# Two states of a scan summed on GpSimd, experts summed in one PSUM bank, and a routing result turned one step later

## The chip, the cores and the metric

The kernel runs on one core of a Trainium2 chip. Its time is device time in microseconds (us) of one execution; three runs of the kernel before gave 5223.3 to 5244.32 us with a median of 5229.83 us. The profile is one further execution. A core has TensorE (PE, matrix products, which write to the accumulator memory PSUM), VectorE (DVE), ScalarE (ACT), GpSimd (POOL) and SyncE (SP, which here issues the DMA transfers). They work side by side, each through its own list of instructions in order, and wait for one another on semaphores. SBUF is the working memory on the chip.

## What is computed

The input x has the shape (4, 128, 64, 64) in fp32: four images of 128 channels and 4096 pixels. Layer 0 normalises, convolves, and runs a selective scan over the pixels of each image. The scan has 16 states for each of its inner channels:

```python
dA = jnp.exp(delta[..., None] * A)
dBu = delta[..., None] * Bm[:, :, None, :] * xin[..., None]
def step(h, inp):
    dA_t, dBu_t, C_t = inp
    h = dA_t * h + dBu_t
    y = jnp.einsum('bdn,bn->bd', h, C_t)      # sum over the 16 states n
    return (h, y)
y = jnp.transpose(ys, (1, 0, 2)) + D_skip * xin
out = y * jax.nn.silu(z) @ out_proj_w.T
```

Layer 1 is attention over the 4096 pixels of an image with 4 heads, followed by a mixture of 8 experts of which the two most probable count:

```python
router_probs = jax.nn.softmax(x @ router_w + router_b, axis=-1)
top_p, top_i = jax.lax.top_k(router_probs, K)                     # K = 2
top_p = top_p / jnp.sum(top_p, axis=-1, keepdims=True)
expert_out = jnp.einsum('bnd,edc->bnec', x, expert_w) + expert_b
gathered = jnp.take_along_axis(expert_out, top_i[..., None], axis=2)
return jnp.einsum('bnk,bnkc->bnc', top_p, gathered)               # added to t
```

## The kernel before

**Tiling.** An image is cut into 8 blocks of 512 pixels (`BLK`, `NB`). Channels lie on the 128 partitions, pixels along the free dimension. For the scan a block has two halves `p` of its channels, and each half has 8 *units* of two states each (`n = 0, 2, ..., 14`): 4 x 8 x 2 x 8 = 512 units. All engine calls go through a helper that keeps the order in which they are written, so nearly every instruction carries line 467 in the profile; the tile names tell them apart.

**The main loop** (line 1322 on) goes in *steps*, called `slot` in the code; a unit takes two, so the scan takes 1024. In the even step of a unit VectorE makes `h<-rows,du` (`driven`, the input of both states, 128x1024) and then the scan `h<-da,state,h` (128x1025, both states in one instruction). In the odd step it makes `hc<-rows,h` (`read`): both states times their row of C. What is left is the sum over the states. It is taken in PSUM: `turned_on` (line 824) turns a term by four transposes of 128x128 on PE, and all terms of a half block are accumulated in the one bank `y`, states and units alike. The list `due` says when: the first term of a unit at the step after its product (`slot + 1`; for the first unit of a half two steps later), the second at `slot + 2`. After the last term ScalarE copies `y`, PE turns it back (`turned_back`), and `summed_up` gates it.

**Attention beside it.** In each step PE also makes the scores `sc<-qs,ks` of one group of keys (four matmuls) and the weighted sums `av<-pT,v` of the group before, and ScalarE makes two exponentials `pT<-sc` of 128x1024. Attention of an image starts as soon as its blocks are closed and outlasts the scan.

**Two lanes.** Everything else is written as generators which are advanced by two stages in each step: lane X runs `closed` (the end of layer 0 of a block) and `finished` (the end of layer 1 of a block, with the experts: an *output*), lane Y runs the norms, the convolution `conv` and `inputs` (the projections that feed the scan). A `yield` ends a stage. Each lane has one PSUM bank, `ps_X` and `ps_Y` (`work(lane)`); `inputs` uses both, and the set `held` says so. An output is started only in certain steps of a block.

**The output** (`finished`, line 1087). After routing on VectorE, whose result is `both` (the shares of the 8 experts, plain and scaled), PE turns `both`, ScalarE copies it to `prT`, and the scaled shares go to DRAM and come back broadcast over the partitions (`share`, two experts at a time, 512 KB). Before the change, `eb8` (the experts' biases times the shares) is made by a matmul in the bank, added with `xf` into `res` on VectorE, and then for every two experts PE makes two matmuls in the bank and VectorE adds the bank to `res`: five VectorE additions of 128x512 an output. There are 32 outputs.

**In steps that are short of work** a stage that must be done by now is forced by `until`, which advances both lanes outside the step order.

Of the kernel before, what the change touches and what calls it, by code (L numbers as in the profile page):

```python
# [24 lines left out]
NST = 16  # L25
DH = 32
NH = 4
NE = 8
# [8 lines left out]
def conv_mamba_attn_moe_kernel(ctx: ExitStack, tc: tile.TileContext, t: dict):  # L37
# [435 lines left out]
    def mm(out, lhsT, rhs, start=True, stop=True):  # L473
        tensor.matmul(out, lhsT=lhsT, rhs=rhs, start=start, stop=stop)
# [8 lines left out]
    def send(out, in_, slots=1):  # L483
        outgoing.append([slots, out, in_])
# [24 lines left out]
    def work(lane, shape=None):  # L509
        return ps_work.tile(shape or [P, BLK], F32, tag=f"work{lane}", name=f"ps_{lane}")  # L510

    def tmp(lane, name, shape=None):
        return side.tile(
            shape or [P, BLK], F32, tag=f"tmp{lane}", name=name, bufs=6 if lane == "X" else 4
        )
# [197 lines left out]
    def inputs(b, i, p):  # L713

        xn, pairs = xn_of[b, i], pairs_of[b, i]
        r = slice(DI * p, DI * p + DI)
        while held:
            yield
            yield
        held.add("in")  # L720
        ps = work("Y")
        summed(ps, [(inxc[:, j, :], pairs[:, p, 2 * j : 2 * j + BLK]) for j in range(2)])
        pz = work("X")
        mm(pz, inz[r, :], xn[r, 3 : 3 + BLK])
        yield
        xin = mix.tile([P, BLK], F32, name="xin", bufs=2)
        scalar.activation(xin, ps, AF.Silu, bias=cb)
        zs = mix.tile([P, BLK], F32, name="zs", bufs=4)
        scalar.activation(zs, pz, AF.Silu)
        yield  # L730

        pb = work("X")
        mm(pb[0:DI, :], wbc, xin)
        ps = work("Y")
        mm(ps, wdt, xin)
        yield
        held.clear()
        bc = tmp("Y", "bc")[0:DI, :]
        scalar.copy(bc, pb[0:DI, :])
        bcd = dram.tile([2, NST // 2, 2, 2 * BLK], F32, name="bcd", bufs=4)  # L740
        send(bcd.rearrange("c n k (m q) -> (c n k m) q", m=2), bc)

        e = tmp("Y", "e")
        scalar.activation(e, ps, AF.Abs, bias=dtb)
        scalar.activation(e, e, AF.Exp, scale=-1.0)
        ln = tmp("Y", "ln")
        scalar.activation(ln, e, AF.Ln, bias=1.0)
        delta = mix.tile([P, BLK], F32, name="delta", bufs=2)
        scalar.activation(delta, ps, AF.Relu, bias=dtb)
        yield  # L750
        yield

        du = mix.tile([P, BLK], F32, name="du", bufs=2)
        lost = du
        vector.tensor_scalar(lost, e, 1.0, -1.0, ALU.add, ALU.add)
        vector.tensor_sub(lost, e, lost)
        vector.tensor_add(ln, ln, lost)
        vector.tensor_add(delta, delta, ln)
        vector.tensor_mul(du, delta, xin)
        in_of[b, i, p] = xin, zs, delta, du, bcd  # L760
        done.add(("in", b, i, p))
        yield
# [324 lines left out]
    def finished(b, qb, lane):  # L1087

        q, u = divmod(qb, 2)
        td = kqv[b][3]  # L1090
        s = slice(qb * BLK, (qb + 1) * BLK)
        acc = side.tile([P, NT, C], F32, name="acc", bufs=2)
        aT, inv = tmp(lane, "aT"), tmp(lane, "inv")
        sync.dma_start(out=aT, in_=total[b, q][u, 0].rearrange("h d q -> (h d) q"))
        sync.dma_start(
            out=inv, in_=inverse[b, q][u][:, None, :].to_broadcast([NH, DH, BLK])
        )
        sync.dma_start(out=acc.rearrange("p j c -> p (j c)"), in_=td[:, s])
        yield
        yield  # L1100
        yield
        vector.tensor_mul(aT, aT, inv)
        yield
        ps = work(lane, [P, NT, C])
        for j in range(NT):
            mm(ps[:, j, :], aT[:, j * P : (j + 1) * P], wp)
        yield
        vector.tensor_add(acc, ps, acc)
        rs = spread(lane, acc)
        yield  # L1110
        ps = transposed(lane, acc)
        yield
        xf = tmp(lane, "xf")
        scalar.copy(xf, ps)
        yield
        ps = work(lane, [P, NT, NE])
        for j in range(NT):
            mm(ps[:, j, :], xf[:, j * P : (j + 1) * P], rw)
        wide = [P, NT, NE]

        def routed(name, n=NE):
            return small.tile([P, NT, n], F32, name=f"{name}{lane}", bufs=1)

        yield

        both = routed("both", 2 * NE)
        pr = routed("pr")
        vector.tensor_mul(pr, ps, rs[:, :, None].to_broadcast(wide))
        vector.tensor_add(pr, pr, rb[:, None, :].to_broadcast(wide))
        m = routed("m", 1)  # L1130
        vector.tensor_reduce(m, pr, AX.X, ALU.max)
        vector.tensor_sub(pr, pr, m.to_broadcast(wide))
        yield
        yield
        scalar.activation(pr, pr, AF.Exp)
        yield
        yield

        revb = rev[:, None, :].to_broadcast(wide)

        def largest(src, tag):
            top, f, pick = routed(f"top{tag}", 1), routed(f"f{tag}", 1), routed(f"pick{tag}")
            vector.tensor_reduce(top, src, AX.X, ALU.max)
            vector.tensor_tensor(pick, src, top.to_broadcast(wide), ALU.is_equal)
            vector.tensor_mul(pick, pick, revb)
            vector.tensor_reduce(f, pick, AX.X, ALU.max)
            vector.tensor_tensor(pick, pick, f.to_broadcast(wide), ALU.is_equal)
            return top, pick

        top1, pick1 = largest(pr, 1)  # L1150
        rest = routed("rest")
        vector.scalar_tensor_tensor(rest, pick1, -2.0, pr, ALU.mult, ALU.add)
        top2, pick2 = largest(rest, 2)
        vector.tensor_add(pick1, pick1, pick2)
        vector.tensor_mul(pr, pr, pick1)
        vector.tensor_add(top1, top1, top2)
        vector.reciprocal(top1, top1)
        vector.tensor_mul(both[:, :, 0:NE], pr, top1.to_broadcast(wide))
        vector.tensor_mul(both[:, :, NE:], both[:, :, 0:NE], rs[:, :, None].to_broadcast(wide))
        yield  # L1160

        ps = work(lane)
        for j in range(NT):
            tensor.transpose(ps[0 : 2 * NE, j * P : (j + 1) * P], both[:, j, :], ident)
        yield
        prT = tmp(lane, "prT")[0 : 2 * NE, :]
        scalar.copy(prT, ps[0 : 2 * NE, :])
        shares = dram.tile([NE, BLK], F32, name=f"shares{lane}")
        send(shares, prT[NE:, :])
        yield  # L1170

        def share(e):

            if lane == "X":
                w = side.tile([P, 2, BLK], F32, name="share", bufs=3)
            else:
                w = mix.tile([P, 2, BLK], F32, tag="rows", name="share", bufs=4)
            sync.dma_start(
                out=w.rearrange("p k q -> p (k q)"),
                in_=shares[e : e + 2].rearrange("e q -> (e q)")[None].to_broadcast([P, 2 * BLK]),  # L1180
            )
            return w


        ps = work(lane)
        mm(ps, eb8, prT[0:NE, :])
        yield
        res = tmp(lane, "res")
        vector.tensor_add(res, ps, xf)
        yield  # L1190
        ahead = deque(share(e) for e in (0, 2))
        yield
        yield
        for e in range(0, NE, 2):
            if e + 4 < NE:
                ahead.append(share(e + 4))
            yield
            w = ahead.popleft()
            if e:
                vector.tensor_add(res, res, ps)  # L1200
            vector.tensor_mul(w, w, xf[:, None, :].to_broadcast([P, 2, BLK]))
            yield
            ps = work(lane)
            for u in range(2):
                mm(ps, ew[:, e + u, :], w[:, u, :], u == 0, u == 1)
        yield
        vector.tensor_add(res, res, ps)
        send(out[b][:, s], res, 2)
        yield


# [86 lines left out]
    groups = attention_groups()  # L1298
    units = [(b, i, p, n) for b, i in blocks for p in range(2) for n in range(0, NST, 2)]
    END = 2 * len(units)  # L1300

    rows, due, closing, y_of = {}, deque(), deque(), {}
    h_of, slot = {}, 0
# [18 lines left out]
    while (  # L1322
# [23 lines left out]
        if unit and odd:  # L1346
            hc = read(h, rows.pop((at, 1)))
            late = 2 * (unit[3] == 0)
            due.append((slot + 1 + late, unit, 0, hc[:, 0, :], False))
            due.append((slot + 2, unit, 1, hc[:, 1, :], ends(unit)))  # L1350
        advance("Y", False)
        while closing and closing[0][0] <= slot:
            summing = turned_back(*closing.popleft()[1:])
# [133 lines left out]
```

## Time and profile before

| | us |
|---|---|
| median of three runs | 5229.83 |
| lowest, highest run | 5223.3, 5244.32 |
| profiled execution, its own time | 5221.24 |
| span of the profile | 5219.4 |

The page has a row for each kind of instruction: how many there were, then their busy time together and the mean duration of one, then the idle time of the engine just before them and what ended it. These rows matter here:

```profile
L467 PE MATMUL y<-ident,hc 128*128 128x128 f32 x4096 | 626.6, 284 | 64.9 <-DVE hc L467 64.9
L467 DVE TENSOR_TENSOR hc<-rows,h 128x1024 f32<-128x1024 f32 x512 | 624.2, 1219 | 16.1 <-PE y L467 5.9
L467 DVE TENSOR_TENSOR res<-res,ps_X 128x512 f32<-128x512 f32 x108 | 73.7, 682 | 51.9 <-PE ps_X L467 51.5
L467 PE MATMUL ps_X<-share,w_ew 128*128 128x512 f32 x432 | 215.5, 622 | 8.7 <-DVE share L467 8.5
```

A matmul's own duration (284 ns for a transpose) is longer than the spacing of two of them, because they are pipelined; 626.6 us for 4096 transposes make 153 ns each. The second part of the page cuts the span into 40 slices of 130 us and gives the busy share of each engine in tenths:

```profile
PE   4566898999999999899999999999999999999997
DVE  4888767777788877888788877888788877751332
ACT  3456787788777777688887787788777787756543
POOL 1111101100000000001000000000000001000000
```

The first slices are the scan of the first blocks, for which there is no attention yet; the scan ends at about 4620 us (the last `y<-ident,hc` starts at 4620.1), and after it attention runs alone, to 5152 us, with the last outputs behind it.

### The profile page before, as it was taken

What the parts mean: (1) busy time and instruction counts of PE and PEld (TensorE: products, weight loads), DVE (VectorE), ACT (ScalarE), POOL (GpSimd) and SP (SyncE); (2) the same over time, 40 slices, a digit from 0 to 9 for tenths busy, and PEclk for the clock granted to TensorE, in tenths of its full rate; (3) what the DMA queues carried; (4) which work ended last, traced back from release to release, by engine and by line L of the source; (5) the groups of instructions that cost most, each with busy time, mean ns of one, the idle gap of its engine ahead of it and who ended that gap; (6) DMA issues with size and microseconds to landing.
All of it is one profiled execution on the core that took longest, in us unless ns stands there. A gap on an engine that the chain in (4) does not pass through costs nothing.

```text
span 5219.4 us, 62693 instructions
## 1 busy us (share of the span) xinstructions
PE 4743.5 (91%) x20704; PEld 2300.7 (44%) x20704; DVE 3834.5 (73%) x5809; ACT 3749.8 (72%) x5701; POOL 423.5 (8%) x483
## 2 busy tenths in 40 slices
PE   4566898999999999899999999999999999999997
PEld 2333444444444444444444444444444444443443
DVE  4888767777788877888788877888788877751332
ACT  3456787788777777688887787788777787756543
POOL 1111101100000000001000000000000001000000
PEclk8677999999999999899999999999999999999998
DMA  3556667767776667767766667767766666754542
GB/s 96 188 186 202 206 215 247 232 231 238 244 231 218 227 227 243 238 232 246 260 230 231 224 223 230 262 227 259 259 236 227 215 230 226 263 181 153 184 134 72
DMA packets 451694, 1131.62 MB, mean 217 GB/s; under 512 B 51985, under 2 KB 135330, under 8 KB 451362
## 3 DMA queue, kind: packets, MB, share of 16 engines
q1 hardware_dynamic: 450194, 1126.74, 64.3%
q8 instruction: 166, 2.72, 0.2%
q14 instruction: 166, 1.36, 0.1%
q10 hardware_dynamic: 1168, 0.80, 0.1%
HBM read 967.12 MB, written 143.39 MB: 213 GB/s over the span
## 4 chain that ended last, share of the span: by engine, by line
PE 55%; DVE 18%; ACT 13%; DMA 6%; issue 5%; POOL 2%; SPq 1%; DVEq 0%; ACTq 0%; POOLq 0%
PE av L467 23%; PE sc L467 13%; PE ps_X L467 8%; DVE h L467 6%; PE ps_Y L467 5%; PE y L467 5%; ACT pT L467 4%; ACT L467 3%; DMA ks<-kd 2%; DVE hc L467 2%; ACT xt L467 1%; ACT e L467 1%; DMA rows<-bcd 1%; DVE stX L467 1%; POOL rsX L467 1%
## 5 line engine op out<-in xcount | busy, mean ns | idle before, releaser
L467 ACT ACTIVATE pT<-sc 128x1024 f32<-128x1024 f32 x2048 | 1984.8, 1023 | 940.1 <-PE sc L467 938.4
L467 PE MATMUL av<-pT,v 128*64 128x512 f32 x8192 | 1998.3, 609 | 12.4 <-DVE avs L467 12.4
L467 PE MATMUL sc<-qs,ks 128*128 128x512 f32 x4096 | 1296.1, 436 | 64.4 <-DMA ks<-kd 32.7
L467 DVE TENSOR_TENSOR_SCAN h<-da,state,h 128x1025 f32<-128x1025 f32 x512 | 1204.2, 2352 | 90.0 <-ACT h L467 56.2
L467 PEld LDWEIGHTS sc<-qs,ks 128*128 128x128 f32 x4096 | 701.3, 190 | 793.3 <-ACT pT L467 261.7
L467 PEld LDWEIGHTS av<-pT,v 128*64 128x64 f32 x8192 | 499.5, 137 | 844.4 <-issue 813.8
L467 ACT ACTIVATE da<-delta,amat 128x512 f32<-128x512 f32 x1024 | 743.0, 730 | 1.9
L467 PE MATMUL y<-ident,hc 128*128 128x128 f32 x4096 | 626.6, 284 | 64.9 <-DVE hc L467 64.9
L467 DVE TENSOR_TENSOR hc<-rows,h 128x1024 f32<-128x1024 f32 x512 | 624.2, 1219 | 16.1 <-PE y L467 5.9
L467 DVE TENSOR_TENSOR h<-rows,du 128x1024 f32<-128x1024 f32 x512 | 623.4, 1218 | 14.2 <-DMA rows<-bcd 13.7
L467 PEld LDWEIGHTS y<-ident,hc 128*128 128x128 f32 x4096 | 520.6, 147 | 235.7 <-issue 83.9
L467 ACT ACT_TABLE_LOAD x319 | 409.3, 1283 | 19.5 <-DVE zs L467 14.3
L467 POOL TENSOR_TENSOR rsX<-rsX,mhalf 128x4 f32<-128x4 f32 x92 | 203.8, 2216 | 2524.6 <-DVE rsX L467 2440.5
L467 POOL TENSOR_TENSOR rsY<-rsY,mhalf 128x4 f32<-128x4 f32 x100 | 130.4, 1304 | 2071.0 <-DVE shiftY L467 1560.3
L467 DVE TENSOR_TENSOR avs<-av,prev 128x512 f32<-128x512 f32 x96 | 66.1, 689 | 252.9 <-PE av L467 238.3
L467 PE MATMUL ps_X<-share,w_ew 128*128 128x512 f32 x432 | 215.5, 622 | 8.7 <-DVE share L467 8.5
L467 ACT ACTIVATE xt<-ps_Y,shiftY,rsY 128x128 f32<-128x128 f32 x380 | 143.8, 469 | 106.4 <-POOL shiftY L467 99.0
L467 DVE TENSOR_TENSOR share<-share,xf 128x1024 f32<-128x1024 f32 x128 | 155.9, 1218 | 15.6 <-DMA share<-sharesX 9.9
L467 ACT COPY state<-h 128x2 f32<-128x2 f32 x448 | 88.7, 198 | 93.5 <-DVE h L467 93.5
L467 DVE SCALAR_TENSOR_TENSOR cm<-y,w_fc1w,cm 128x512 f32<-128x512 f32 x192 | 142.8, 744 | 3.4
L467 PE MATMUL ps_Y<-pairs,inxc 128*128 128x512 f32 x256 | 129.2, 629 | 15.6 <-DMA pairs<-xn 10.3
L467 PEld LDWEIGHTS ps_X<-share,w_ew 128*128 128x128 f32 x432 | 73.6, 190 | 146.8 <-issue 98.5
(254 smaller groups left out, 3455.8 us busy)
## 6 DMA issues: line engine op xcount, KB each, us to landing
rows<-bcd SPq DMA_DIRECT2D x1024, 512.0 KB
ks<-kd SPq DMA_DIRECT2D x192, 512.0 KB
qs<-qd SPq DMA_DIRECT2D x161, 512.0 KB
share<-sharesX SPq DMA_DIRECT2D x108, 512.0 KB
v<-vd SPq DMA_DIRECT2D x192, 256.0 KB
ks<-kd SPq DMA_DIRECT2D x128, 256.0 KB
avd<-avs SPq DMA_DIRECT2D x96, 256.0 KB
prev<-avd SPq DMA_DIRECT2D x96, 256.0 KB
```

What stands on the lines that cost most here:

```text
L467: return lambda *args, **kw: queued(op(*args, **kw))
```

## The change

The edit has three parts.

1. *Two states.* From step 64 on (`ALONE = NB // 2 * NST`), GpSimd adds the two halves of the product `hc` in place, a 128x512 addition, and PE turns and accumulates one term for each unit instead of two. The term is due at `slot + 2` (for the first unit of a half at `slot + 3`). In the first 64 steps all is as before. So 480 of the 512 units have the addition.
2. *Experts in one bank.* The bias matmul `eb8` and the eight experts' matmuls are accumulated in one PSUM bank in one go; VectorE adds `xf` once at the end. Between the first and the last of them lane X keeps its bank: it puts `"mix"` into `held`, for which `inputs` waits, and before it does so it waits itself until `held` is empty.
3. *Shares later.* Two more stages, one step, lie between the routing on VectorE and the transposes of its result on PE.

```diff
@@ inputs @@
-        held.clear()
+        held.discard("in")
@@ finished @@
         vector.tensor_mul(both[:, :, NE:], both[:, :, 0:NE], rs[:, :, None].to_broadcast(wide))
         yield
-
+        yield
+        yield
         ps = work(lane)
...
-        ps = work(lane)
-        mm(ps, eb8, prT[0:NE, :])
-        yield
-        res = tmp(lane, "res")
-        vector.tensor_add(res, ps, xf)
+        yield
         yield
         ahead = deque(share(e) for e in (0, 2))
         yield
         yield
+        while lane == "X" and held:
+            yield
+            yield
+        if lane == "X":
+            held.add("mix")
+        ps = None
         for e in range(0, NE, 2):
             if e + 4 < NE:
                 ahead.append(share(e + 4))
             yield
             w = ahead.popleft()
-            if e:
-                vector.tensor_add(res, res, ps)
             vector.tensor_mul(w, w, xf[:, None, :].to_broadcast([P, 2, BLK]))
             yield
-            ps = work(lane)
+            if e == 0:
+                ps = work(lane)
+                mm(ps, eb8, prT[0:NE, :], True, False)
             for u in range(2):
-                mm(ps, ew[:, e + u, :], w[:, u, :], u == 0, u == 1)
-        yield
-        vector.tensor_add(res, res, ps)
+                mm(ps, ew[:, e + u, :], w[:, u, :], False, e + u == NE - 1)
+        yield
+        res = tmp(lane, "res")
+        vector.tensor_add(res, ps, xf)
         send(out[b][:, s], res, 2)
+        held.discard("mix")
         yield
@@ main loop @@
+    ALONE = NB // 2 * NST
...
             late = 2 * (unit[3] == 0)
-            due.append((slot + 1 + late, unit, 0, hc[:, 0, :], False))
-            due.append((slot + 2, unit, 1, hc[:, 1, :], ends(unit)))
+            if slot < ALONE:
+                due.append((slot + 1 + late, unit, 0, hc[:, 0, :], False))
+                due.append((slot + 2, unit, 1, hc[:, 1, :], ends(unit)))
+            else:
+                gpsimd.tensor_add(hc[:, 0, :], hc[:, 0, :], hc[:, 1, :])
+                due.append((slot + 2 + late // 2, unit, 0, hc[:, 0, :], ends(unit)))
```

## The prediction

> **What bounds the kernel now.** I read four views in this order: the page's first table, the busy table cut into stretches of one block, the waits inside those stretches, and the timeline of GpSimd against VectorE.
>
> ```profile
> PE 4743.5 (91%) x20704; PEld 2300.7 (44%) x20704; DVE 3834.5 (73%) x5809; ACT 3749.8 (72%) x5701; POOL 423.5 (8%) x483
> ```
>
> TensorE (PE) leads, but an average over the span cannot say what an edit is worth. A block of 512 pixels is 16 units of the scan (two halves of eight). I cut the block that begins at 2708.30 at the starts of its products hc: two units, seven units, seven units.
>
> ```profile
> 2708.30:2734.13 25.83, 25.83 (x116) 12.59 (x116) 13.21 (x19) 22.96 (x33) 0.00 (x0) 1.00 0.54 182
> 2734.13:2796.05 61.92, 59.78 (x273) 29.39 (x270) 58.99 (x93) 44.63 (x74) 5.07 (x8) 1.00 0.66 225
> 2796.05:2853.20 57.15, 55.73 (x257) 26.82 (x256) 45.42 (x67) 49.50 (x77) 6.54 (x6) 1.00 0.71 233
> ```
>
> Columns: stretch, length, then busy us of PE, weight loads, DVE (VectorE), ACT, POOL (GpSimd). In the first and third stretch PE is busy 100% and 97.5% of the time and VectorE 51% and 79%: PE sets the time. In the middle one both are full, VectorE at 95%, PE at 97%. The waits agree; the first two lines below are VectorE's from the first stretch, the next from the middle one (PE's), the last two from the third:
>
> ```profile
> DVE acc L467 <- PE ps_X L467: 8.5, 1, 8.5
> DVE xin L467 <- PE y L467: 2.7, 1, 2.7
> ...
> PE ps_X L467 <- DVE bothX L467: 2.1, 1, 2.1
> ...
> DVE hi L467 <- PE ps_X L467: 5.8, 2, 3.4
> DVE vst L467 <- PE ps_X L467: 3.3, 1, 3.3
> ```
>
> Outside the middle stretch VectorE runs ahead and waits for PE. Inside it VectorE's listed waits are only 1.3 us (0.7 for a res, 0.6 for a cm), and PE waits 2.1 us for the routing result bothX. The middle stretch is therefore VectorE's: what loads VectorE there lengthens it, and what relieves PE there gains nothing.
>
> **The one thing the trace must tell: GpSimd against VectorE.** The new add reads two SBUF operands on GpSimd. The kernel before has no such add, but it has small GpSimd operations beside large VectorE ones:
>
> ```profile
> 2605.96 0.24 POOL L467 COPY y<-y 128x64 f32<-128x64 f32 x1
> ...
> 1149.38 1.15 POOL L467 COPY y<-y 128x64 f32<-128x64 f32 x1
> ...
> 1149.22 1.22 DVE L467 TENSOR_TENSOR h<-rows,du 128x1024 f32<-128x1024 f32 x1
> ...
> 2807.55 1.99 POOL L467 TENSOR_TENSOR rsX<-rsX,mhalf 128x4 f32<-128x4 f32 x1 [1.96 <-DVE shiftX L467]
> ...
> 2807.45 1.22 DVE L467 TENSOR_TENSOR hc<-rows,h 128x1024 f32<-128x1024 f32 x1
> 2808.59 1.22 DVE L467 TENSOR_TENSOR h<-rows,du 128x1024 f32<-128x1024 f32 x1
> ```
>
> The same copy takes 0.24 us alone and 1.15 us when h<-rows,du is running: it ends 0.09 us after that product. The power 128x4 takes 1.01 us alone (at 4636.01) and 1.99 us when it meets hc. Since 0.87 us of it follow hc's end while the next product is already started, GpSimd gets in between two VectorE instructions that follow each other.
>
> [...] that VectorE waits for GpSimd no instruction of this trace shows[...]. [...] COPY 128x64 at 0.24 and COPY 128x3 at 0.18 us make 0.98 ns an element, twice that for two operands, so 1.0 us and 0.18 of start. I take a hold of 1.1 us, with ends 0 (VectorE is not held) and 1.9 us.
>
> **The change part by part.**
>
> The sum of two states. 480 of the 512 units (all but the first 64 steps, 32 units) lose four transposes. At 2741.07 four of them start and the next av starts at 2741.60, so 0.53 us of PE a unit (busy time says 626.6/4096 x 4 = 0.61, ends overlapping). In the first and third stretch, PE's own, that is 9 x 0.53 = 4.8 us a block. VectorE has room there: it is busy 13.2 + 45.4 of 83.0 us, and nine holds add at most 9.9. In the middle stretch the 3.7 us of PE are worth nothing.
>
> There the hold counts. I laid one add behind each of the seven hc of that stretch in the timeline[...]: behind du<-e 1.1; behind gn [...] 0.8; behind h, delaying the scan, 1.0; beside the first tap cm 0.65; then 1.05 three times, delaying a tap or an h. Sum 6.7 us on a VectorE without slack.
>
> The term is due at step +2 instead of +1 and +2. The add is done 1.2 to 2.3 us after hc, a step lasts 145/32 = 4.5 us, so PE's transposes do not wait; if that cover went, each late add would cost PE its lateness. Powers queued behind an add need statistics which VectorE makes after hc anyway (4 x 0.28 us and more): nothing, or up to 1.1 us each on ACT's xt where this fails. The product buffer hc is freed at the same step +2.
>
> Experts in one bank. For each of the 32 outputs VectorE loses five 128x512 adds and gains one. In the middle stretch: res<-ps_X,xf 0.69 and four res<-res,ps_X 2.7 go, one 0.69 comes, and the 0.7 wait before the first goes: 3.4 us off VectorE. PE's matmuls are the same; eb8 moves behind the first share. The bank is held by lane X during the mix and the `inputs` stage waits for it: in the instruction order of the two kernels the matmuls of `inputs` stand at the same step or one earlier, so nothing waits.
>
> Shares a step later. Two stages more between routing and transposes. It takes away PE's 2.1 us for bothX (45.9 us over the span), but in VectorE's stretch: 0, at most those 46 us. One extra step of lane X has room.
>
> **Sum for a block with an output:** middle 6.7 - 3.4 - 0.6 (the wait for PE at its end) = +2.7; others -4.8; together -2.1. For 23 such blocks -48. Five blocks (554 to 1244 us) have no output and so no adds to lose; there VectorE has 4.5 of 60.0 us idle to take up the holds (1127.90 to 1187.89): +4 - 4.8 = -0.8 each, -4. The two blocks between 310 and 554 us, where PE is busy 72% and VectorE 81%: 0 to +25, I take +11. The tail: both last outputs run eb8 (2.07 and 1.91 us at 5190.79 and 5192.66) before the shares arrive, now after: +3. Total -38 us: 5221.2 - 38 = 5183 against the profiled execution, which is 8.6 us under the median; so 5192 for the median.
>
> **Rivals.**
>
> A. VectorE is hardly held [...]. Then the middle stretch follows PE, which loses 3.7 and 2.1, and VectorE, which loses 3.4: -3.2; others -4.8; -8.0 in 23 blocks, about -6.8 in the five without an output, tail +3: -215, 5015. For it: no VectorE instruction in the trace is seen held. Against it: GpSimd is held fully in the other direction.
>
> B. Slower: the add holds VectorE longer than estimated, because it is slower itself or because each delayed VectorE instruction also delays its next partner. Place: the middle stretch; price: 6.7 x hold/1.1. The sum of a block changes sign at 6.7 x hold/1.1 = 4.8 + 4.0, a hold of 1.44 us. At 1.9 us it is +11.6 - 4.0 - 4.8 = +2.8 in 23 blocks (+64), +4.1 in the five others (+20), +20 at the start, +3 at the tail: 5337. For it: 95% busy VectorE with nothing to absorb. [...]
>
> C. The add comes late and PE waits for it, so that the unit is as long as before: half of the 4.8 us is gone in 28 blocks, 67 us: 5259. For it: PE waits for hc today, 64.9 us over the span. Against it: two steps of slack.
>
> **How the numbers follow.** Main case 0.50 (holds of 0.9 to 1.45 us give -3.3 to 0 a block, with the other terms -75 to +25 us: 5155 to 5255), A 0.17, B 0.24, C 0.09. A measurement of this kernel can tell about 0.5%, 26 us, from no change. Faster: 0.31 of the main case and all of A, 0.48; slower: B, 0.07 of C and 0.04 of the main case, 0.35; the rest, 0.17, within. Since both signs hold much, the main case's range stands above; the range for 8 in 10 reaches into A and B, 5050 to 5290.
>
> **What would show it.** Four transposes a unit fewer (about 2176 y<-ident,hc instead of 4096) and a new POOL row hc<-hc x480 at 1.1 us alone, 1.5 to 2.5 us with its wait. VectorE rows such as scan, h or the taps longer, or idle before them released by POOL, some 0.8 us a unit: if these are unchanged and the stretches of 62 us get shorter, A. PE's share in the middle stretch falls to about 88% and the stretch grows to 64 or 65 us; the rest of a block shrinks from 83.0 to 78 us. PE waits for bothX vanish. I am wrong if the middle stretch passes 67 us (B) or PE's waits for POOL before y exceed some 50 us (C).

## The result and the profile after

The change makes the kernel slower by 1.0%: 5286.18 us (5280.59 to 5287.42) against 5235.17 us for four runs of the kernel before (5223.3 to 5244.32; three of them are those of the section on the time before), ratio 1.0097 with a 95% interval of 1.0073 to 1.0121. The profiled execution has a span of 5283.8 us, 64 us more than before.

The first table of the page after the change:

```profile
PE 4630.3 (88%) x18784; PEld 2103.8 (40%) x18784; DVE 4039.5 (76%) x5681; ACT 3752.7 (71%) x5701; POOL 1350.8 (26%) x963
```

PE did lose its work: 1920 matmuls and 113 us. VectorE has 128 instructions fewer and yet 205 us more. The groups of instructions say where those come from (columns: count, then busy us in total and ns of one, then idle us before):

```profile
L467 POOL TENSOR_TENSOR hc<-hc 128x512 f32<-128x512 f32 x480 | 868.3, 1809 | 2294.1 <-DVE hc L467 2207.4
L467 DVE TENSOR_TENSOR_SCAN h<-da,state,h 128x1025 f32<-128x1025 f32 x512 | 1349.2, 2635 | 70.0 <-ACT h L467 36.6
L467 DVE TENSOR_TENSOR h<-rows,du 128x1024 f32<-128x1024 f32 x512 | 689.8, 1347 | 6.7 <-DMA rows<-bcd 6.7
L467 DVE SCALAR_TENSOR_TENSOR cm<-y,w_fc1w,cm 128x512 f32<-128x512 f32 x192 | 185.6, 967 | 3.4
L467 PE MATMUL y<-ident,hc 128*128 128x128 f32 x2176 | 355.9, 293 | 66.7 <-DVE hc L467 36.9
L467 PE MATMUL ps_X<-share,w_ew 128*128 128x512 f32 x432 | 235.2, 670 | 45.7 <-DVE share L467 45.6
```

Before, the scan took 2352 ns, h<-rows,du 1218 and the tap cm 744. Of VectorE's idle time only 15.9 us are put down to GpSimd, and 11.9 before: a VectorE instruction that is held shows as a longer one, not as a wait. One unit of the middle stretch shows it, first on VectorE's timeline (start, duration), then on GpSimd's:

```profile
3394.90 1.22 DVE L467 TENSOR_TENSOR h<-rows,du 128x1024 f32<-128x1024 f32 x1
3396.23 3.17 DVE L467 TENSOR_TENSOR_SCAN h<-da,state,h 128x1025 f32<-128x1025 f32 x1
3399.60 1.22 DVE L467 TENSOR_TENSOR hc<-rows,h 128x1024 f32<-128x1024 f32 x1 [0.20 <-POOL y L467]
3400.74 0.54 DVE L467 TENSOR_SCALAR cm<-y,w_fc1w,w_fc1b 128x512 f32<-128x512 f32 x1
3401.32 1.66 DVE L467 SCALAR_TENSOR_TENSOR cm<-y,w_fc1w,cm 128x512 f32<-128x512 f32 x1
```

```profile
3395.13 2.12 POOL L467 TENSOR_TENSOR hc<-hc 128x512 f32<-128x512 f32 x1 [3.50 <-DVE hc L467]
...
3400.91 1.52 POOL L467 TENSOR_TENSOR hc<-hc 128x512 f32<-128x512 f32 x1 [1.48 <-DVE hc L467]
```

The first addition starts while h<-rows,du runs and ends at 3397.25, 1.13 us after that product (3396.12); it takes 2.12 us, where the shortest of the 480 takes 1.26. The scan, started 0.11 us after the product, takes 3.17 us instead of 2.35. The second addition meets the tap cm, which takes 1.66 us instead of 0.74. The tap with one tile operand ahead of it keeps its 0.54 (all 24 of the span take 0.52 to 0.54).

Now the stretches of one block (columns as in the prediction, then PE's clock, DMA share, GB/s): first the kernel before, then the same block after.

```profile
3307.93:3329.53 21.60, 21.60 (x99) 10.56 (x99) 13.20 (x19) 20.88 (x29) 0.00 (x0) 1.00 0.75 210
3329.53:3391.47 61.94, 59.75 (x273) 29.40 (x270) 58.98 (x93) 43.97 (x67) 5.07 (x8) 1.00 0.64 217
3391.47:3448.18 56.71, 55.36 (x256) 26.66 (x254) 45.43 (x68) 48.61 (x70) 6.51 (x7) 1.00 0.69 233
```

```profile
3352.56:3372.87 20.31, 20.17 (x86) 9.34 (x88) 14.92 (x21) 19.04 (x27) 5.63 (x7) 1.00 0.59 191
3372.87:3437.81 64.94, 60.07 (x245) 27.32 (x242) 60.99 (x87) 44.84 (x68) 19.42 (x15) 0.95 0.62 219
3437.81:3498.71 60.90, 59.08 (x254) 26.48 (x254) 50.84 (x70) 52.85 (x76) 19.67 (x14) 1.00 0.69 225
```

The middle stretch is 3.0 us longer, as forecast. The third, which should have become shorter, is 4.2 us longer, and PE is busier in it by 3.7 us although it turns seven terms less: work has come into it from elsewhere. In the middle stretch PE has 28 instructions fewer, is busy no less, and its clock has sunk to 0.95.

This 0.95 comes from two short pieces at half the clock. Here is the first, on PE's timeline and then as a stretch of its own (columns as above):

```profile
3388.39 1.94 PE L467 MATMUL av<-pT,v 128*64 128x512 f32 x8
...
3393.23 0.66 PE L467 MATMUL ps_Y<-ident,xt 128*128 128x128 f32 x4 [1.77 <-ACT xt L467]
3393.81 3.39 PE L467 MATMUL av<-pT,v 128*64 128x512 f32 x8
```

```profile
3394.16:3397.56 3.40, 3.40 (x11) 0.77 (x8) 3.30 (x3) 3.10 (x6) 2.43 (x4) 0.50 0.36 117
```

PE waits 1.77 us for xt; ahead of the statistics for this xt VectorE had an h<-rows,du that took 2.30 us (at 3384.24) instead of 1.22. About 0.9 us after the wait PE's clock is at half for 3.41 us, and the eight matmuls of av take 3.39 us instead of 1.94. The second piece, from 3414.63 on, follows a wait of 2.17 us for an expert's share. In the 22 blocks of the table at the end, PE's time at half clock is 236 us after the change and 89 before.

PE's waits after the change:

```profile
PE sc L467 <- DMA ks<-kd: 56.7, 28, 6.0
PE sc L467 <- ACT pT L467: 54.3, 137, 2.6
PE ps_X L467 <- DVE share L467: 45.6, 17, 4.8
...
PE y L467 <- POOL hc L467: 28.3, 6, 8.4
```

The waits for bothX are down to 8.8 us from 45.9, and the one for the experts' shares has come (8.5 before). PE's wait for the added term is small, 28.3 us.

### The profile page after: what moved, and what is told of

The parts are those of the page before. It is cut to its first block, busy times and chain, and to the rows that moved or that the text cites. A ratio compares the mean times of both kernels' runs of the same rounds, so it can differ in the third digit from the quotient of the medians.

```text
span 5283.8 us, 59904 instructions
## 1 busy us (share of the span) xinstructions
PE 4630.3 (88%) x18784; PEld 2103.8 (40%) x18784; DVE 4039.5 (76%) x5681; ACT 3752.7 (71%) x5701; POOL 1350.8 (26%) x963
## 3 DMA queue, kind: packets, MB, share of 16 engines
q1 hardware_dynamic: 450194, 1126.74, 63.6%
## 4 chain that ended last, share of the span: by engine, by line
PE 47%; DVE 23%; ACT 12%; DMA 7%; issue 7%; POOL 2%; SPq 1%; DVEq 0%; POOLq 0%; ACTq 0%
PE av L467 20%; PE sc L467 11%; DVE h L467 10%; PE ps_X L467 8%; PE ps_Y L467 5%; ACT pT L467 4%; ACT L467 3%; DMA ks<-kd 3%; DVE hc L467 3%; PE y L467 3%; DVE cm L467 1%; ACT xt L467 1%; DVE du L467 1%; DVE stX L467 1%; SPq L467 1%
## 5 line engine op out<-in xcount | busy, mean ns | idle before, releaser
L467 PE MATMUL av<-pT,v 128*64 128x512 f32 x8192 | 2024.7, 616 | 40.5 <-DVE avs L467 40.2
L467 POOL TENSOR_TENSOR hc<-hc 128x512 f32<-128x512 f32 x480 | 868.3, 1809 | 2294.1 <-DVE hc L467 2207.4
L467 PE MATMUL sc<-qs,ks 128*128 128x512 f32 x4096 | 1320.0, 441 | 113.2 <-DMA ks<-kd 56.7
L467 DVE TENSOR_TENSOR_SCAN h<-da,state,h 128x1025 f32<-128x1025 f32 x512 | 1349.2, 2635 | 70.0 <-ACT h L467 36.6
L467 DVE TENSOR_TENSOR h<-rows,du 128x1024 f32<-128x1024 f32 x512 | 689.8, 1347 | 6.7 <-DMA rows<-bcd 6.7
L467 ACT ACT_TABLE_LOAD x319 | 409.3, 1283 | 21.1 <-DVE zs L467 15.9
L467 PE MATMUL y<-ident,hc 128*128 128x128 f32 x2176 | 355.9, 293 | 66.7 <-DVE hc L467 36.9
L467 POOL TENSOR_TENSOR rsY<-rsY,mhalf 128x4 f32<-128x4 f32 x100 | 148.6, 1486 | 1037.1 <-DVE shiftY L467 552.0
L467 PEld LDWEIGHTS y<-ident,hc 128*128 128x128 f32 x2176 | 292.2, 152 | 187.3 <-issue 62.0
L467 PE MATMUL ps_X<-share,w_ew 128*128 128x512 f32 x432 | 235.2, 670 | 45.7 <-DVE share L467 45.6
L467 DVE SCALAR_TENSOR_TENSOR cm<-y,w_fc1w,cm 128x512 f32<-128x512 f32 x192 | 185.6, 967 | 3.4
```

The lines of the kernel that those rows point to most:

```text
L467: return lambda *args, **kw: queued(op(*args, **kw))
```

## The experiments

Times are medians; those of the kernel before, measured beside the four sets, were 5237.7, 5236.7, 5238.5 and 5233.2. "Middle" is units 2 to 8 of a block, "outer" units 0, 1 and 9 to 15. The table at the end gives the mean lengths of both.

**First set: which part costs?**

*The additions alone*: the main loop of the change, with `finished` and `inputs` as before. Of the parts put back:

```diff
-        yield
-        yield
         ps = work(lane)
...
+        mm(ps, eb8, prT[0:NE, :])
...
+            if e:
+                vector.tensor_add(res, res, ps)
...
-                mm(ps, ew[:, e + u, :], w[:, u, :], False, e + u == NE - 1)
+                mm(ps, ew[:, e + u, :], w[:, u, :], u == 0, u == 1)
```

> GpSimd's sum of the two states alone, the experts and their shares as before the change. Theory H (each GpSimd add holds VectorE up[...]): VectorE gets the holds without the additions it loses in the changed kernel, so slower than the changed kernel, 5310 to 5360 us. Theory M (the mix in one bank and the shares a step later cost the time, TensorE waiting for the first share): the add shows its gain of about 4.8 us a block, 5080 to 5150 us. Theory L (TensorE gets its term too late from GpSimd, whatever VectorE does): about as the changed kernel, 5280 us, with TensorE waiting for GpSimd's hc.

5291.22 us, ratio 1.0097 (1.0075 to 1.0118). The additions by themselves give the whole loss, and theory M falls. The number is nearest to theory L's, but PE waits only 16.8 us for GpSimd's hc; H had the direction and too much of it.

*The experts' edits alone*: the main loop of before with the two other parts.

```diff
-            if slot < ALONE:
-                due.append((slot + 1 + late, unit, 0, hc[:, 0, :], False))
-                due.append((slot + 2, unit, 1, hc[:, 1, :], ends(unit)))
-            else:
-                gpsimd.tensor_add(hc[:, 0, :], hc[:, 0, :], hc[:, 1, :])
-                due.append((slot + 2 + late // 2, unit, 0, hc[:, 0, :], ends(unit)))
+            due.append((slot + 1 + late, unit, 0, hc[:, 0, :], False))
+            due.append((slot + 2, unit, 1, hc[:, 1, :], ends(unit)))
```

> Experts in one bank and shares a step later alone, two terms for a unit as before the change. H: VectorE loses about 2.7 us a block and nothing holds it, TensorE's wait for bothX is gone: faster than before by 20 to 90 us, 5145 to 5215. M: slower than before by 50 us or more, 5285 and up. L: as H.

5246.3 us, ratio 1.0017 (1.001 to 1.0023). No theory had that: 80 us less of VectorE (3754.2) bring no time. The same block shows where they go:

```profile
3319.07:3340.24 21.17, 21.04 (x94) 10.20 (x96) 13.18 (x20) 20.31 (x30) 1.35 (x5) 1.00 0.68 205
3340.24:3400.79 60.55, 59.05 (x269) 29.03 (x266) 55.32 (x86) 43.72 (x67) 5.54 (x8) 1.00 0.67 227
3400.79:3460.33 59.54, 57.64 (x263) 27.61 (x263) 46.75 (x69) 48.88 (x70) 6.69 (x7) 1.00 0.68 223
```

VectorE does 3.7 us less in the middle, which is 1.4 us shorter, and 1.3 us more in the third stretch, which is 2.8 us longer, with 2.3 us more of PE. By tile names, what moved are the stages of lane X behind the output, a unit later: tt<-ps_X,rsX,xr, stX<-tt and ps_X<-w_projT,cm go from unit 9 to unit 10. PE's waits move likewise: over the span those for bothX are 2.5 us instead of 45.9, but those for hc are 94.6 instead of 64.9 and those for the keys 44.3 instead of 32.7.

*No addition*: the one term that is turned is the first state's.

```diff
-                gpsimd.tensor_add(hc[:, 0, :], hc[:, 0, :], hc[:, 1, :])
```

> The changed kernel with GpSimd's add left out: one term a unit is turned, the other states' terms are missing from the output. TensorE has all of the relief, VectorE no hold, TensorE no wait for GpSimd. H and L: 5010 to 5070 us. M: above 5130, since the mix still costs.

5150.98 us, ratio 0.9836 (0.9812 to 0.986). So additions cost 135 us, but 480 units' relief of PE brings only 95 us against the experts' edits alone, much less than theories H and L expected. The number is one that M allows, but the experts' edits, M's cause, cost only the 9 us of the run before.

*Waiting for GpSimd without its reading*: the addition is replaced by two writes of zeros.

```diff
-                gpsimd.tensor_add(hc[:, 0, :], hc[:, 0, :], hc[:, 1, :])
+                gpsimd.memset(hc[:, 0, :], 0.0)
+                gpsimd.memset(hc[:, 0, :], 0.0)
```

> The changed kernel with two GpSimd memsets of the term in place of the add (the terms are then zero): TensorE still waits for about 1.1 us of GpSimd work behind each product, but GpSimd reads nothing. H: as without the add, within 25 us of it, with scan, h and tap durations back to 2.35, 1.22 and 0.74 us. L: near the changed kernel, 5250 us and more. M: as the changed kernel.

5163.95 us, ratio 0.9856 (0.9836 to 0.9876). That TensorE gets its term from GpSimd costs 13 us, theory L's share; the other 122 us come with what the addition reads. An addition also lasts longer than the two writes (1.81 us on average against 1.07), but PE's waits for the term differ by only 6 us (28.3 and 22.1). The groups of this kernel:

```profile
L467 POOL MEMSET hc<- 128x512 f32 x960 | 513.9, 535 | 2521.9 <-DVE hc L467 2410.1
L467 DVE TENSOR_TENSOR h<-rows,du 128x1024 f32<-128x1024 f32 x512 | 623.9, 1219 | 11.0 <-DMA rows<-bcd 10.9
```

These 960 GpSimd instructions write SBUF and read nothing, and they leave h<-rows,du at its 1219 ns, the scan at 2353 and the tap at 744.

**Second set: where does a hold cost, and how does it grow?**

*Additions in the outer units alone*, and then *in the middle alone*, each from the change:

```diff
-            if slot < ALONE:
+            if slot < ALONE or 2 <= at % 16 <= 8:
```

```diff
-            if slot < ALONE:
+            if slot < ALONE or not 2 <= at % 16 <= 8:
```

> The change, but the units 2 to 8 of each block keep two terms and no addition; the other nine have it (270 additions instead of 480). Base of all sums: the kernel with the experts' edits alone, 5246, from which 480 terms less took 95 us and 480 holds then gave 135. Theory P (place: holds cost time only in the middle stretch, where VectorE is full, and relief of PE is worth something only outside it): all the relief and no hold, 5150 to 5195, faster than before. Theory E (everywhere: a hold costs the same in every unit, and so does the relief): 9/16 of both, 5246 - 53 + 76 = 5269, 5255 to 5280.

> The complement: additions only in units 2 to 8 of each block, two terms and no addition in the other nine (210 additions). P: no relief that counts and all of the holds' price, 5246 + 135 = 5381, at least 5320. E: 7/16 of both, 5246 - 42 + 59 = 5263, 5250 to 5280. If both this kernel and its complement lie under the full change, the price of holds grows faster than their number; if their two differences from 5246 add up to the full change's 40, it is linear in it.

Outer alone 5198.15 us, ratio 0.9923 (0.9903 to 0.9942), faster than before; middle alone 5347.01 us, ratio 1.0207 (1.019 to 1.0224). E falls, and P holds in kind: the first lies 3 us above its range, the second 34 us below its sum. Measured from 5246.3 they are -48 and +101; their sum, +53, stands near the full change's +40, so the two places hardly interact. One block of the outer, then of the middle kernel, second stretch alone:

```profile
3318.35:3378.90 60.55, 59.09 (x269) 29.19 (x266) 55.33 (x86) 44.57 (x68) 5.56 (x8) 1.00 0.66 232
```

```profile
3410.55:3475.55 65.00, 59.66 (x245) 27.16 (x242) 60.64 (x87) 43.84 (x67) 19.47 (x15) 0.95 0.63 217
```

5.3 us more of VectorE for seven additions and 4.45 us more of length; 24 matmuls fewer gave PE nothing: its busy time is no shorter (59.66 us against 59.09), at the lower clock.

*One operand instead of two*: GpSimd copies.

```diff
-                gpsimd.tensor_add(hc[:, 0, :], hc[:, 0, :], hc[:, 1, :])
+                gpsimd.tensor_copy(hc[:, 0, :], hc[:, 1, :])
```

> GpSimd copies the second state's term over the first instead of adding the two (in units with the addition the first state's term is missing from the output and the second stands alone). It reads one operand instead of two. If the hold is as long as what GpSimd reads, VectorE is held about half as long and the time lies halfway between no hold (5151, or 5164 with the wait) and the change (5286): 5215 to 5235. If a GpSimd instruction with one operand doesn't hold VectorE at all: about 5165. If it is the write, or any use of the tile, that holds: 5270 to 5290.

5189.59 us, ratio 0.991 (0.9893 to 0.9926), between the first two cases. The groups:

```profile
L467 DVE TENSOR_TENSOR h<-rows,du 128x1024 f32<-128x1024 f32 x512 | 644.0, 1258 | 10.6 <-DMA rows<-bcd 10.5
...
L467 POOL COPY hc<-hc 128x512 f32<-128x512 f32 x480 | 550.9, 1148 | 2421.6 <-DVE hc L467 2351.6
```

VectorE's total is 3822.4 us against 3753.6 without any GpSimd work on hc, 0.14 us for each copy; the additions made it 4039.5, 0.60 us each. A hold grows faster than the bytes read, and the expectation of half was wrong. Against the writes of zeros, the copy costs 26 us.

*The addition twice.*

```diff
                 gpsimd.tensor_add(hc[:, 0, :], hc[:, 0, :], hc[:, 1, :])
+                gpsimd.tensor_add(hc[:, 0, :], hc[:, 0, :], hc[:, 1, :])
```

> Two GpSimd additions in a row for each unit (the second state's term counts twice in the output). Theory H (the hold is what costs): 135 us more, 5390 to 5450, and scan, h and taps on VectorE longer again by some 0.6 us an addition. Theory L (TensorE waits for the late term): PE's wait for hc from GpSimd rises from 40 us by several hundred, the time likewise to 5450 or more, with VectorE's durations as they are. If holds are taken up by slack: under 5310.

5495.16 us, ratio 1.0489 (1.0472 to 1.0507): 209 us more, above what H expected. VectorE's total rises by 276 us (4315.3), 0.57 us for each addition more, so the hold is about the same; but PE's wait for the term also rises, to 145.9 us from 28.3. The first addition of a unit costs 0.25 us of time (122/480), the second 0.44. Slack that takes up a part of the first would do that, and so would PE's longer wait; this run does not part the two.

**Third set: what became of the relief?**

*The nine outer units relieved without additions* (two terms in the middle), with the new experts' edits.

```diff
-            if slot < ALONE:
+            if slot < ALONE or 2 <= at % 16 <= 8:
...
-                gpsimd.tensor_add(hc[:, 0, :], hc[:, 0, :], hc[:, 1, :])
```

> As the kernel with additions in the nine outer units of a block, but without these additions (in those units the second state's term is missing from the output); units 2 to 8 keep two terms. It tells the relief of the outer units from their holds. If the holds outside the middle cost nothing, it is as fast as with them, 5190 to 5205, and TensorE's relief there is worth 48 us and no more. If they cost as much as the rest of the 135, 34 us, it is at about 5164, and the relief outside is 82 of the 95 us. The prediction took 134 us for the relief: 5112.

5183.02 us, ratio 0.9893 (0.9876 to 0.991). Outer holds cost 15 us (5183 to 5198), which is hardly clear of the noise; the outer relief is worth 63 us against the experts' edits alone, not the 134 of the prediction.

*Outer additions with the experts as before*, and *additions in units 0, 1 and 8 to 12 with the experts as before*. From the additions alone:

```diff
-            if slot < ALONE:
+            if slot < ALONE or 2 <= at % 16 <= 8:
```

```diff
-            if slot < ALONE:
+            if slot < ALONE or not (at % 16 < 2 or 8 <= at % 16 <= 12):
```

> Additions in the nine outer units alone, and the experts and their shares as before the change: a version meant to beat both. If the parts add up (experts' edits cost 9 us), 5198 - 9 = 5189, 5180 to 5200. If the experts' edits help once additions are there (with all the additions the full change was 5 us faster than the additions alone), 5200 to 5210.

> Additions in units 0, 1 and 8 to 12 alone, experts as before the change. In units 13 to 15 of a block VectorE is at 94% and the pitch of a unit rose with the addition by 0.4 to 0.7 us each. If what counts is whether VectorE is full in that unit, leaving these three out gains their 1.8 us a block and loses at most 1.6 us of TensorE's relief that comes late, in units 0 and 1 of the next block: 5175 to 5195. If TensorE's relief counts wherever it comes, since its backlog is carried from units 13 to 15 into 0 and 1: 5205 to 5225.

5175.48 us, ratio 0.988 (0.9862 to 0.9898), and 5213.62 us, ratio 0.9956 (0.9939 to 0.9973). The first beats both kernels, by more than the sum expected. The second is 38 us slower than the first. It also adds in unit 8, which lengthens its middle by 0.5 us, 15 us over 30 blocks; the other 23 us are what the rest of a block loses when units 13 to 15, where VectorE had looked full, are left out (81.3 to 81.8 us a block in the table, so 15 us of them are seen there). What the additions cost in these units is regained in units 0 and 1 of the next block, which last 20.9 us with them and 23.6 without (means of 22 blocks), presumably because PE comes to them with less in arrears. A stretch is not a closed account.

*One bank alone*: the experts' sum, without the two later stages. From the experts' edits alone:

```diff
         vector.tensor_mul(both[:, :, NE:], both[:, :, 0:NE], rs[:, :, None].to_broadcast(wide))
         yield
-        yield
-        yield
         ps = work(lane)
```

> The experts' sum in one bank alone: no addition of two states, and the shares at the step of before. In the kernel with both experts' edits the middle stretch was 1.7 us shorter and the rest of a block 2.2 us longer than before, with VectorE's work in units 10 and 12 up by 2.8 us and in units 4 to 6 down by 2.5. Theory S (the shares a step later push the rest of the output's lane into the third stretch): without the later shares the middle stretch keeps its gain and the rest is 83 us again, 5180 to 5210. Theory B (the bank that is kept during the mix, and inputs behind it, pushes the work): 5240 to 5260, as with both.

5232.9 us, ratio 0.9992 (0.9982 to 1.0002). Neither number was met. The third stretch is at its old length, so it was the later shares that moved work there (theory S's reason); but the middle keeps its old length too, although VectorE does less in it. The bank that lane X keeps does not explain that: the products of `inputs` and, but for one block of 22, the stages behind the output stand in the units where they were before. So VectorE's relief alone buys nothing there, and the 1.7 us by which both experts' edits shorten the middle are work moved out of it.

**Fourth set: what eats the outer relief?** Silu, Gelu and Ln replaced by Relu in the kernel before, then in the kernel with the outer relief and no additions.

```diff
-        scalar.activation(xin, ps, AF.Silu, bias=cb)
+        scalar.activation(xin, ps, AF.Relu, bias=cb)
-        scalar.activation(zs, pz, AF.Silu)
+        scalar.activation(zs, pz, AF.Relu)
...
```

> The kernel before with the Silu, Gelu and Ln activations of ScalarE replaced by Relu (so the convolution's, gate's and step's nonlinearities are other ones in the output), which leaves the exponentials' table loaded: 319 table loads of 1.28 us, 409 us of ScalarE's 3750, go. It is the control of the next run. If TensorE alone sets the time outside the middle, it is within 30 us of before, 5205 to 5235; if ScalarE is the limit in unit 1 and in units 11 and 12, 5100 to 5180.

> The same replacement in the kernel that drops the second state's term in the nine outer units (no additions). Theory A (ScalarE is what keeps the rest of TensorE's relief): the relief against the control is near the predicted 134 us, at least 100. Theory N (ScalarE is not it): it stays 40 to 70 us under the control.

5198.47 us, ratio 0.9933 (0.9916 to 0.9949), and 5132.34 us, ratio 0.9811 (0.9795 to 0.9828). The first lies between the two ranges expected for it. The difference is 66 us, against 55.5 between the same two kernels with their table loads: theory A falls. With 400 us less of ScalarE, PE's wait for pT is 17.2 us instead of 54.6 in the same kernel with its table loads, but those for hc and for the keys are 92.4 and 60.1 instead of 85.3 and 54.0: the next limit is close behind.

*The outer relief, no additions, experts as before.* From the outer additions with the experts as before:

```diff
-                gpsimd.tensor_add(hc[:, 0, :], hc[:, 0, :], hc[:, 1, :])
```

> The second state's term dropped in the nine outer units, no additions, experts and shares as before the change. With additions the like kernel took 5175. If a hold outside the middle costs 15 us as with the new experts: 5160, and the relief there is 78 us. If the experts' edits had eaten the relief: 5100 to 5120.

5157.05 us, ratio 0.9862 (0.9846 to 0.9879): the relief is 76 us. This kernel differs from before by 1080 transposes and the step of the term that is left, so its account can be read from two groups, whose lines before were y x4096 at 626.6 us and sc with 64.4 us of idle time ahead of it:

```profile
L467 PE MATMUL sc<-qs,ks 128*128 128x512 f32 x4096 | 1303.9, 437 | 114.0 <-ACT pT L467 61.3 <-DMA ks<-kd 51.8 <-ACT da L467 0.4
L467 PE MATMUL y<-ident,hc 128*128 128x128 f32 x3016 | 477.3, 287 | 53.1 <-DVE hc L467 53.1
```

The transposes gave up 149 us of their own. 50 us come back as PE's idle time before the scores: waiting for ScalarE to empty their bank (pT, 30.5 to 61.3) and for the keys' loads (32.7 to 51.8). The other 23 us between 149 and 76 are not settled; PE's total falls by 107 us, not by 149, since the busy times of such rows overlap with their neighbours' (before, the rows of PE's matmuls sum to 5225 us, and PE's total is 4743.5).

*The version put together from this*: outer additions, one bank, shares at their old step. From the change:

```diff
-        yield
-        yield
         ps = work(lane)
...
-            if slot < ALONE:
+            if slot < ALONE or 2 <= at % 16 <= 8:
```

> Additions in the nine outer units, experts in one bank, but the shares at the step of before. One bank alone took 6 us off and the outer additions alone 63. If they add up: 5170, 5160 to 5178, the fastest of the whole kernels. If the step-later shares are not what cost 23 us beside the outer additions: 5190 to 5200.

5164.69 us, ratio 0.9873 (0.9856 to 0.9889), the fastest kernel that computes everything, 1.3% faster than before. Its interval overlaps that of outer additions alone (0.9862 to 0.9898), so that the one bank adds something is not shown.

Mean lengths in us over 22 blocks (8 to 29), cut at the starts of hc:

| kernel | middle | outer | time |
|---|---|---|---|
| before | 63.4 | 83.2 | 5235 |
| after | 66.2 | 82.9 | 5286 |
| additions alone | 68.7 | 80.9 | 5291 |
| experts' edits alone | 61.8 | 85.4 | 5246 |
| one bank alone | 63.6 | 83.2 | 5233 |
| outer additions, new experts | 61.9 | 83.7 | 5198 |
| middle additions, new experts | 66.3 | 85.1 | 5347 |
| outer relief without additions, new experts | 61.7 | 82.9 | 5183 |
| outer relief without additions, old experts | 63.4 | 80.5 | 5157 |
| outer additions, old experts | 63.5 | 81.3 | 5175 |
| outer additions, one bank | 63.1 | 81.1 | 5165 |
| additions in 0, 1, 8 to 12, old experts | 64.0 | 81.8 | 5214 |

## Why the prediction was wrong

It said 5192 us and the kernel takes 5286: inside the range of 5050 to 5290, on the wrong side. The mechanism, that GpSimd's addition holds VectorE up and that this lengthens the middle stretch, was right. Two credits that were set against it failed, and the loss through PE's clock was not in the sum at all. By runs, from before to after:

| term | predicted, us | measured, us | from which runs |
|---|---|---|---|
| both experts' edits | -89 | +9 | before to the experts' edits alone |
| PE's relief outside the middle | -134 | -63 | from there to the outer relief without additions |
| holds outside the middle | 0 | +15 | from there to the outer additions |
| PE's relief in the middle | 0 | -32 | outer relief without additions to no addition |
| additions in the middle | about +185 | about +120 | the 135 us of all additions less the 15 |
| sum | -38 | +49 | the whole change measured +51 |

- *The experts in one bank* ("3.4 us off VectorE", with 0.6 for VectorE's wait for PE, in 23 blocks: -92 us) is the first step that failed. The prediction itself gave PE 97% in that stretch, yet took it for VectorE's alone. One bank alone left the middle at 63.6 us and the time at -0.1%: with PE as full, less work for VectorE alone brought no time.
- *The shares a step later* were costed at 0 and "one extra step of lane X has room": that failed too. PE's wait for bothX went as foretold, but lane X's next stages are pushed out of the middle, which becomes 1.7 us shorter, into the third stretch: +2.2 us a block outside. Both experts' edits together miss their credit by 98 us.
- *PE's relief outside the middle* ("PE's own, that is 9 x 0.53 = 4.8 us a block", -134 us): the 0.53 us are right, but at most 2.7 us a block arrive. That PE was "busy 100%" said that nothing else was later at that moment, not that there were 4.8 us of room behind it: the banks of the scores and the keys' loads are next at once. With the experts moved in it was 63 us, without them 76. This miss of 71 us would turn the sign as the 98 us do, each by itself.
- *The hold* (6.7 us for seven in a block): right in kind, and too large. It was the author's estimate; no VectorE instruction of the trace before was seen held. An addition takes 1.26 us at its shortest, more than the estimate of 1.18 from the small copies, and a held instruction gets up to 1.1 us longer (the longest scan 3.38 us, h 2.31, tap 1.67). But the seven cost VectorE 5.3 us in the block shown, 0.76 each, so not every addition holds one up for its whole length. The middle grows by 4.3 us (61.9 to 66.2) or 5.2 (63.5 to 68.7).
- *The middle's length* was right by luck: "the stretch grows to 64 or 65 us", +2.8 on average against +2.7, since a smaller hold met a smaller credit for the experts. "What relieves PE there gains nothing" failed: 32 us.
- *PE's clock* has no term in the prediction. Time at half clock in the 22 blocks is 89 us before, 130 without the additions, 157 with the writes of zeros and 236 after. Half of the last difference, 79 us, is 39 us of PE's work, an estimate of the most that PE lost to it in these blocks, beside the 122 us that the additions cost over the writes of zeros in all. No run holds the clock fixed, so its share stays open.
- *VectorE has room outside*: nearly. Outer holds cost 15 us, or 9 to 18 with the old experts (5157 to 5175, in two sets), not 0.
- *The term a step later*: 13 us in the kernel with zeros written, and 28.3 us of PE's waits; below the 50 that would have meant rival C.
- *The two early blocks*: 249.5 us after, 243.9 before, so +5.6 of the +11 taken.

Of the rivals C, 5259, came nearest in time, then B, 5337, and neither for its reason: PE hardly waited for GpSimd, the middle reached 66.2 us and not 67 or more, and the hold was shorter than 1.44 us, not longer.

## What to carry to other kernels

Where two engines are at 95% and 97% in a stretch, less work for one of them need not bring time, and more work for it costs: here VectorE's relief alone brought no time clear of the noise (0.9982 to 1.0002), and PE's relief in the same stretch brought 32 us in a kernel where VectorE was relieved too. Credit what relieves both, and look up what the freed engine waits for next. Before an operation goes to GpSimd, list what VectorE runs at that moment, and place it by stretch: the same addition, with the relief that it brings, was worth -48 us in nine units of sixteen and +101 in the other seven. A stage that is moved a step later takes all stages behind it along; ask into which stretch they fall.

## What the runs showed of the hardware

- A VectorE instruction that GpSimd holds shows no wait: it becomes longer by up to 1.1 us, and VectorE's idle time put down to GpSimd hardly changes (15.9 us against 11.9).
- In these runs the price rose with what GpSimd reads, more than in proportion: per instruction of 128x512 VectorE lost 0.60 us to an addition of two operands and 0.14 us to a copy, and beside the writes of zeros its h<-rows,du, scan and tap kept their 1219, 2353 and 744 ns.
- More idle time of PE and a lower clock came together. PE's idle time in a block rose from 7.2 to 12.9 us (mean of the same 22 blocks), its time at half clock in these blocks from 89 to 236 us, and the whole span's granted clock was 0.941 after and 0.958 before. The two pieces at half clock named above, 3.41 us each, began 0.9 and 0.8 us after waits of 1.77 and 2.17 us. Not every wait of that length is followed by one: before the change 20 of the 38 waits over 1.5 us in those blocks neither lay in a piece at half clock nor had one within the next 5 us.
